# A planned transformer stack on one core: margins on landings, other luck numbers, waits for single pieces of preparation, later preparation of later layers

## The chip, the cores and the metric

The kernel runs on one core of one Trainium2 chip. The core has five engines with queues of their own: TensorE (PE, with its weight loads PEld), VectorE (DVE), ScalarE (ACT), GpSimd (POOL) and SyncE (SP), which here issues the DMAs. Each engine works off its queue in order; an instruction that waits for a semaphore holds up all that stand behind it. The metric is the time of one execution on the device in microseconds (us); the median of several runs is compared.

## The reference

The input x has 128 sequences of 64 tokens with 128 features; ctx has the same shape; cond is 128 by 128. Four layers of a conditioned transformer follow one another, all in fp32, with 16 heads of 8 features. In short:

```python
def adaln(x, scale, shift): return (1 + scale) * norm(x) + shift      # scale, shift from silu(cond) @ W + b

# layer 0: cross attention to ctx
x = x + attn(adaln(x), adaln(ctx)) @ Wp + bp
# layer 1: gated self attention, cross attention, gated GELU MLP
x = x + g1 * (self_attn(adaln(x)) @ W_proj + b)
x = x + cross_attn(norm(x), norm(ctx)) @ W_cproj + b
x = x + g2 * (gelu(adaln(x) @ W_mlp1 + b) @ W_mlp2 + b)
# layer 2: gated self attention, gated cross attention, gated SwiGLU MLP
x = x + g3 * (self_attn(adaln(x)) @ w_so + b)
s, i = top_k(scores(adaln(x), ctx), 16)            # 16 of 64 keys for each query and head
x = x + g4 * (softmax(s) @ v[i] @ w_co + b)
x = x + g5 * ((silu(a) * b) @ w_m2 + b_m2)         # a, b = adaln(x) @ w_m1 + b_m1
# layer 3: as layer 1
```

## The kernel before

The 128 sequences are cut into 16 chunks of 8 (512 tokens). Eight lanes each work on one chunk at a time, so the chunks go through in two waves. The function `chunk` writes down all steps of one chunk as operations: an engine, a cost in nanoseconds, the tiles that it writes and reads, a latency for a DMA, and a closure that issues the instructions.

One attention goes like this. A norm (statistics on DVE, L698; root on POOL, L711 and L712; normalisation on DVE, L719) is turned by PE (L686) and scaled on DVE (L728) and shifted on POOL (L729). PE makes keys (pk, L751), queries (pq, L757) and values (pv, L775), which ACT evicts. Four DMAs spread the queries (qbd, `spread`) so that PE can compute scores head by head (L809; for the top-k attention L839). ACT takes the exponential (L820), PE gathers the values (po, L939), ACT copies the result out (L949), and it takes a return trip through DRAM: store, load of the sums (`cs`), reciprocal on DVE (L974), store, broadcast load (`rb`), product on POOL (L984). Then PE makes the output product (py, L1049), which goes to the residual, with a gate that is fetched from DRAM by token (`by_token`). In the top-k attention DVE searches the 16 largest of 64 (L877, L879, L881), POOL masks (L907) and PE turns the result (ppt, L915). An MLP has products ph or pa and pg (L1071) and py (L1062).

The order of the instructions on every engine is made by the class `Plan` while the program is built. It keeps a clock for each engine, and at each turn gives out, of the operations within a window of each lane, the one that could start first; ties and near ties are moved by a jitter of 1% on each cost (`near`), drawn from the 21 numbers in `LUCK`, one for each 350 turns. An operation's start also takes in buffers (`start`; the pool `some` of 30 tiles, 3 query buffers, 4 value buffers, 8 probability buffers, PSUM banks), a table switch on ACT, a half-rate PE after idle stretches (`work`), the port that DVE and POOL share, DMAs that are still moving (`moves`, `moving`: each recent DMA adds its share to the landing of a new one) and the fetch of PE's code in blocks (`late`: before, the mean over eight phases of 256 instructions with a fetch of 3,400 ns, and for the small products of scores and gathers alone). `in_turn` then pins the order of each queue. Where the plan sees PE idle for over 1,000 ns ahead of a fresh PSUM tile, it issues filler matmuls over half of that time (`warm`, L1219 before), whose results are overwritten.

`prepare` is planned together with the lanes: it clears the query and value buffers on POOL, loads and turns the biases and the condition, makes the scales and shifts (pm, L532, L539), loads the weights (L557, L572; some are reordered on DVE, L391), the plain biases (pb, L508, L502, L579) and the gates (pg, L591; copies L598 to L601), which are stored in DRAM once (L609) and copied there in a 1 MB broadcast (L612). Each layer has a mark `ready[layer]`: a planned step without instructions that needs all parts of that layer, and `wop` lets each of the lane's steps that read weights wait for the mark. Preparation of layers 2 and 3 waits, in the plan, for the mark two layers earlier. Neither these marks nor the plan's times are instructions: on the chip a step waits for the tiles that it really reads.

At the end a count decides whether a second, slower network must run; it does not with these inputs.

Of the kernel before, what the change touches and what calls it, by code (L numbers as in the profile page):

```python
# [11 lines left out]
ALU = mybir.AluOpType  # L12
# [17 lines left out]
    14171, 51121, 34343, 55919, 69, 91271, 28258, 26931, 84363, 82916, 66128,  # L30
    83140, 28802, 5022, 44198, 77867, 32905, 75983, 99066, 65698, 73229,
# [68 lines left out]
PE, DVE, ACT, POOL, SP = "PE", "DVE", "ACT", "POOL", "SP"  # L100
# [30 lines left out]
class Plan:  # L131
# [15 lines left out]
    FETCH = 3400.0  # L147
    SHORT, LONG = 1500.0, 3500.0

    def __init__(self, tc, slots, warm, luck):  # L150
        self.tc, self.last, self.warm, self.luck = tc, {}, warm, luck
        self.count, self.chosen = 0, 0
        self.size = slots
        self.free = {kind: [(0.0, k) for k in range(n)] for kind, n in slots.items()}
        self.made, self.next_turn = {}, {}
        self.engine_free = dict.fromkeys((PE, DVE, ACT, POOL, SP), 0.0)
        self.port, self.active = {DVE: (0.0, 0.0), POOL: (0.0, 0.0)}, {}
        self.ops, self.holds, self.moving = None, None, []
        self.table = None
        self.small, self.blocks = 0, [(k, -self.FETCH) for k in range(0, self.BLOCK, 32)]  # L160
# [15 lines left out]
    def op(self, engine, cost, outs, ins, give, latency=0.0, bulk=False, table=None, small=0, within=False, port=False, moves=None, rate=1.0):  # L176
# [8 lines left out]
        o.moves, o.rate = moves, rate  # L185
# [12 lines left out]
    def start(self, o, first=True):  # L198
# [28 lines left out]
        if o.small:  # L227
            at += self.late(o, at)
# [17 lines left out]
    def late(self, o, at, keep=False):  # L246


        total = 0.0
        for k, (used, asked) in enumerate(self.blocks):  # L250
            waits, n = 0.0, o.small
            while used + n >= self.BLOCK:
                n -= self.BLOCK - used
                there = at + waits + o.cost * (1 - n / o.small)
                waits += max(0.0, asked + self.FETCH - there)
                used, asked = 0, max(there, asked + self.FETCH)
            total += waits
            if keep:
                self.blocks[k] = used + n, asked
        return total / len(self.blocks)  # L260
# [15 lines left out]
    def give_out(self, o, at):  # L276
# [19 lines left out]
        if fresh and idle > self.IDLE:  # L296
            self.work(at - idle, idle / 2)
        self.table = o.table or self.table
        if o.engine == PE:
            self.small = o.small  # L300
            if o.small:
                self.late(o, at, True)
# [7 lines left out]
        o.end = over + o.latency  # L310
        if o.moves:
            self.moving = [(t, n) for t, n in self.moving if over - t < self.LONG]
            o.end += sum(n[over - t >= self.SHORT] for t, n in self.moving)
# [32 lines left out]
    def run(self, lanes, count, ahead=()):  # L346
# [4 lines left out]
        while True:  # L351
# [9 lines left out]
            for n, ops in enumerate(todo):  # L361
                for i, (c, o) in enumerate(ops[: self.WINDOW]):
                    if o.missing or best and max(o.ready, self.engine_free[o.engine]) > best[0][0]:
                        continue
                    at = self.start(o, c == oldest or o.within)
# [13 lines left out]
def kernel(ctx: ExitStack, tc: tile.TileContext, ins: dict, out: bass.AP, nchunk: int = NCHUNK):  # L379
# [57 lines left out]
    def prepare(plan, ready, all_of_it, vblocks, queries, pool, spills):  # L437
# [7 lines left out]
        def clear(kind, cost, give):  # L445
            t = plan.tile(lambda: None, kind)
            op(POOL, cost, [t], [], lambda: give(t.slot))
            return t
# [6 lines left out]
        cleared = [clear("qbd", 1800, lambda k: nc.gpsimd.memset(queries[k], 0.0)) for _ in range(plan.size["qbd"])]  # L455
        cleared += [clear("values", 1500, clear_values) for _ in range(plan.size["values"])]
        if not all_of_it:
            op(SP, 1, ready, cleared, lambda: None)
# [26 lines left out]
        op(PE, 400, [ph], [bi, mb], turn_biases)  # L485
        op(DVE, 600, [biases], [ph], keep_biases)
        pc = mm("pc")
# [7 lines left out]
        op(PE, 220, [pc], [th], lambda: nc.tensor.transpose(pc()[:, :P], th(), ident))  # L495
# [15 lines left out]
        for layer in range(4):  # L511
            of, late = f"L{layer}", layer > 1
            dma, queue = (nc.sync, SP) if late else (nc.scalar, ACT)
            parts, weights, behind = cleared if layer == 0 else [], {}, [ready[layer - 2]] if late else []


            for key, wname, bname, kinds in CONDS:
# [3 lines left out]
                for i0 in range(0, len(kinds), 4):  # L521
# [5 lines left out]
                    ), 3500, bulk=late)  # L527
# [14 lines left out]
                    if those:  # L542
                        op(PE, 223 * len(those), [p], [cw, sc], products, bulk=late)
                        op(DVE, 350 * len(those), [done], [p, biases], keep, bulk=late)
                        parts.append(done)
                    weights[key, i0] = cw
# [3 lines left out]
            for name, k, n in WEIGHTS:  # L550
# [3 lines left out]
                ready_w[name] = whole = plan.kept(True)  # L554
                if m:
# [3 lines left out]
                    ), 3000, bulk=late)  # L559
# [7 lines left out]
                    parts.append(part)  # L567
                if m < n:
# [3 lines left out]
                    op(queue, 450, [whole], behind, lambda of_w=of_w, to=to: dma.dma_start(out=to, in_=of_w), 3000, bulk=late)  # L572
                    parts.append(whole)

            for name, w, b, bv in PLAIN:
                if name.startswith(of):
                    p, done = mm("pb"), plan.kept(True)
                    op(PE, 450, [p], [ready_w[w], bi, biases], lambda p=p, w=w, b=b, bv=bv: added(p()[:, :D], w, b, bv), bulk=late)
                    op(ACT, 300, [done], [p], lambda p=p, name=name: nc.scalar.copy(plain[name], p()[:, :D]), bulk=late)  # L579
                    parts.append(done)  # L580

            for n, (key, i, w, b, bv) in enumerate(GATES):
# [18 lines left out]
                op(PE, 900, [p], [cw, sc, bi, biases, *([ready_w[w]] if w else [])], products, bulk=late)  # L603
# [13 lines left out]
                ), 6000, bulk=late)  # L617
                parts.append(done)

            op(SP, 1, [ready[layer]], parts, lambda: None)  # L620
# [14 lines left out]
    def lane(n, plan, work, safe, acc, ready, vblocks, queries, pool, spills):  # L635
# [4 lines left out]
        op, layer = plan.op, [0]  # L640

        def wop(engine, cost, outs, takes, *rest, **how):

            op(engine, cost, outs, [*takes, ready[layer[0]]], *rest, **how)
# [35 lines left out]
        def flip(x, name):  # L680
# [7 lines left out]
            op(PE, 510, [p], [x], turn, rate=0.75)  # L688
# [38 lines left out]
        def modulate(h, pn, scale, shift, c):  # L727
            wop(DVE, 620, [h], [pn], lambda: nc.vector.tensor_tensor(b3(h()), b3(pn()), by_batch(scale, c), ALU.mult))  # L728
# [4 lines left out]
        def ln(x, eps, scale=None, shift=None, c=None):  # L733
# [5 lines left out]
            else:  # L739
                modulate(h, pn, scale, shift, c)  # L740
            return h, mv

        def attention(hq, hkv, wq, bq, wk, wv, topk=False):
# [7 lines left out]
            wop(PE, 890, [pk], [hkv], lambda: nc.tensor.matmul(pk(), lhsT=wk, rhs=hkv(), start=True, stop=True))  # L751
# [5 lines left out]
            wop(PE, 890, [pq, qbd, taken], [hq], lambda: nc.tensor.matmul(pq(), lhsT=wq, rhs=hq(), start=True, stop=True))  # L757

            qT = some([P, T])
            op(ACT, 670, [qT, qbd], [pq], lambda: nc.scalar.activation(qT(), pq(), AF.Identity, bias=bq))  # L760
# [16 lines left out]
            wop(PE, 930, [pv, vbuf], [hkv, taken], values)  # L777
# [48 lines left out]
            def weigh_rows(i, prs):  # L826
# [83 lines left out]
                for half, ex in enumerate(exs):  # L910
# [9 lines left out]
                    op(PE, 475, [ppt], [ex], turn, rate=0.75)  # L920
# [86 lines left out]
        def by_token(n, part, c, behind):  # L1007
# [9 lines left out]
            wop(SP, 590, [g], behind, fetch, 2690, moves=(395, 244))  # L1017
            return g

        def add(x, gate, c, parts):  # L1020

            if isinstance(gate, str):
                wop(POOL, 1265, [x], [x], lambda: nc.gpsimd.tensor_tensor(
# [18 lines left out]
        def project(oT, w, x, gate, c):  # L1042
# [3 lines left out]
            def product():  # L1046
                for t in range(NT):
                    cols = slice(t * P, (t + 1) * P)
                    nc.tensor.matmul(py()[:, cols], lhsT=oT()[:, cols], rhs=w, start=True, stop=True)  # L1049

            wop(PE, 960, [py], [oT], product)
            residual(py, x, gate, c, oT.behind)

        def mlp_out(gs, w2, x, gate, c):
# [3 lines left out]
            def sum_up():  # L1058
                for t in range(NT):
                    cols = slice(t * P, (t + 1) * P)  # L1060
                    for j in range(NJ):
                        nc.tensor.matmul(  # L1062
                            py()[:, cols], lhsT=gs[j // 2]()[:, j % 2, cols], rhs=w2[:, j, :], start=(j == 0), stop=(j == NJ - 1)
                        )

            wop(PE, 3610, [py], gs, sum_up)
            residual(py, x, gate, c, gs[1])

        def product(w, j, h, name, *takes):
            p = mm(name)  # L1070
            wop(PE, 890, [p, *takes], [h], lambda: nc.tensor.matmul(  # L1071
                p(), lhsT=w[:, j * P : (j + 1) * P], rhs=h(), start=True, stop=True
# [3 lines left out]
        def gelu_mlp(h, w1, b1, w2, x, gate, c):  # L1076
            gs = [shared([P, NJ // 2, T], "prob") for _ in range(2)]

            def part(j):
                ph = product(w1, j, h, "ph", *([] if j else gs))  # L1080
                op(ACT, 690, [gs[j // 2]], [ph], lambda: nc.scalar.activation(
# [7 lines left out]
        def swiglu_mlp(h, w1, b1, w2, x, gate, c):  # L1089
# [3 lines left out]
            def part(j):  # L1093
                pa = product(w1, j, h, "pa", *([] if j else gs))
                z, w = some([P, T]), some([P, T])
                op(ACT, 690, [z], [pa], lambda: nc.scalar.activation(z(), pa(), AF.Identity, bias=bvec(b1, j)))
                op(ACT, 580, [w], [pa], lambda: nc.scalar.activation(
# [14 lines left out]
        def chunk(c):  # L1112
            def qkv(w, b):
                w = W[w]
                return w[:, 0:D], bmix(b), w[:, D : 2 * D], w[:, 2 * D : 3 * D]

            def q_kv(wq, bq, wkv):
                w = W[wkv]
                return W[wq], bmix(bq), w[:, 0:D], w[:, D : 2 * D]
# [3 lines left out]
            def scaled(key, scale, shift):  # L1123
                return mods[key, scale], mods[key, shift], c
# [24 lines left out]
            layer[0] = 0  # L1149
# [5 lines left out]
            project(o, W["L0_xcond_Wp"], x, "L0", c)  # L1155

            layer[0] = 1
# [4 lines left out]
            project(o, W["L1_xcond_W_proj"], x, 0, c)  # L1162
# [4 lines left out]
            project(o, W["L1_xcond_W_cproj"], x, "L1c", c)  # L1167
            h, mv = ln(x, 1e-6, *scaled("L1", 4, 3))
            add(x, 1, c, mv)
            gelu_mlp(h, W["L1_xcond_W_mlp1"], "L1_xcond_b_mlp1", W["L1_xcond_W_mlp2"], x, 1, c)  # L1170

            layer[0] = 2
# [5 lines left out]
            project(o, W["L2_xcond_w_so"], x, 2, c)  # L1178
# [6 lines left out]
            project(o, W["L2_xcond_w_co"], x, 3, c)  # L1185
            h, mv = ln(x, 1e-6, *scaled("L2", 7, 6))
            add(x, 4, c, mv)
            swiglu_mlp(h, W["L2_xcond_w_m1"], "L2_xcond_b_m1", W["L2_xcond_w_m2"], x, 4, c)

            layer[0] = 3  # L1190
# [4 lines left out]
            project(o, W["L3_xcond_sa_proj_w"], x, 5, c)  # L1195
# [4 lines left out]
            project(o, W["L3_xcond_ca_proj_w"], x, "L3c", c)  # L1200
            h, mv = ln(x, 1e-6, *scaled("L3", 4, 3))
            add(x, 6, c, mv)
            gelu_mlp(h, W["L3_xcond_fc1_w"], "L3_xcond_fc1_b", W["L3_xcond_fc2_w"], x, 6, c)
# [7 lines left out]
    def network(lanes, safe, acc=None):  # L1211
# [13 lines left out]
        def planned(luck, tc=None, work=None, *tiles):  # L1225
            plan = Plan(tc, slots, warm, luck)
            tiles, ready = tiles or (None,) * 4, [plan.kept(True) for _ in range(4)]
# [74 lines left out]
```

## Time and profile before

| | |
|---|---|
| median of 3 runs | 1819.86 us (1807.23 to 1823.54) |
| the profiled execution | 1828.91 us |
| its span | 1827.1 us |
| its mean granted PE clock | 0.967 |
| DMA queue's bytes | 260.87 MB, 143 GB/s on average |

In the lines further down, a group's line has its line in the code, engine, operation, the tile written and the tiles read. A row of waits names the waiting engine, line and tile, then what ended the wait, with the total in us, the number of waits and the longest. The slices cut the span into 40 equal parts of 45.7 us with a busy share in tenths.

### The profile page before, as it was taken

The numbers are of one execution on the slowest core, as the hardware profiler recorded it, in microseconds if no ns is written. First come the engines' busy times: TensorE is split into PE (matmuls) and PEld (weight loads), VectorE is DVE, ScalarE is ACT, GpSimd is POOL, SyncE is SP. The second block draws the span as 40 slices with busy tenths as digits, with TensorE's granted clock in tenths as the row PEclk, the third lists the DMA queues.
The fourth block names the chain that finished last, engine by engine and source line by source line (L and its number), as shares of the span: only waits on it lengthen the run. The fifth ranks groups of instructions, "written<-read, shape, count | busy, mean of one in ns | idle before, by whom it ended". The sixth has DMA issues, their size and how long they took to land. (4 is left out here: it accounts for less than half of the span.)

```text
span 1827.1 us, 74911 instructions
## 1 busy us (share of the span) xinstructions
PE 1642.7 (90%) x30403; PEld 1149.1 (63%) x30403; DVE 1282.8 (70%) x6075; ACT 1248.3 (68%) x1824; POOL 1123.9 (62%) x1306
## 2 busy tenths in 40 slices
PE   6689999998887999998999999999999989889987
PEld 4456666666555666666666667676666666666665
DVE  5633344698999995966873596998684889996522
ACT  0477777587555777676777877787587768676562
POOL 6655465736655675755775666766666656576533
PEclk8899999999989999998999999999999999999999
DMA  8646655346422445446455545536354553345442
GB/s 248 190 143 183 174 161 158 104 131 184 115 68 84 119 125 157 146 142 180 132 157 156 152 128 174 166 117 176 102 162 141 149 149 112 114 123 144 118 142 85
DMA packets 296822, 260.87 MB, mean 143 GB/s; under 512 B 53196, under 2 KB 216212, under 8 KB 296468
## 3 DMA queue, kind: packets, MB, share of 16 engines
q1 hardware_dynamic: 296468, 255.99, 48.3%
q8 instruction: 242, 3.96, 1.0%
q14 instruction: 112, 0.92, 0.2%
HBM read 154.83 MB, written 79.04 MB: 128 GB/s over the span
## 5 line engine op out<-in xcount | busy, mean ns | idle before, releaser
L820 ACT ACTIVATE prob<-ps 128x1024 f32<-128x1024 f32 x384 | 375.4, 1024 | 86.2 <-PE ps L809 85.1
L939 PEld LDWEIGHTS po<-prob,vbuf 128*32 128x32 f32 x14336 | 221.3, 113 | 103.1 <-issue 56.1
L939 PE MATMUL po<-prob,vbuf 128*32 128x64 f32 x14336 | 262.3, 225 | 15.0 <-issue 10.7
L719 DVE TENSOR_SCALAR some<-x,parts,rstd 128x128 f32<-128x128 f32 x640 | 200.3, 376 | 66.0 <-POOL rstd L712 65.7
L907 POOL TENSOR_TENSOR some<-some,some 128x512 f32<-128x512 f32 x128 | 162.8, 1275 | 124.7 <-ACT some L899 80.7
L809 PE MATMUL ps<-qbd,some 32*64 32x256 f32 x6144 | 227.4, 393 | 11.0 <-DMA qbd<-some 5.7
L984 POOL TENSOR_TENSOR some<-some,some 128x512 f32<-128x512 f32 x112 | 143.2, 1279 | 125.8 <-DMA some<-spillrec 32.6
L712 POOL TENSOR_TENSOR rstd<-rstd,minus_half 128x4 f32<-128x4 f32 x192 | 201.6, 1050 | 16.0
L879 DVE MATCH_REPLACE8 some<-m,some 128x64 f32<-128x64 f32 x1024 | 206.5, 209 | 0.3 <-issue 0.3
L1037 POOL TENSOR_TENSOR x<-x,some 128x512 f32<-128x512 f32 x112 | 143.6, 1284 | 85.1 <-DVE some L1036 64.7
L782 ACT COPY vbuf<-pv 64x512 f32<-64x512 f32 x224 | 153.9, 687 | 44.8 <-PE pv L775 42.8
L877 DVE MAX8 m<-some 128x8 f32<-128x64 f32 x1024 | 172.0, 209 | 16.0 <-ACT some L857 15.8
L881 DVE MAX8 m<-some 128x8 f32<-128x64 f32 x1024 | 177.1, 215 | 0.0
L949 ACT COPY some<-po 128x512 f32<-128x512 f32 x224 | 132.0, 589 | 64.0 <-PE po L939 46.4
L1028 POOL TENSOR_TENSOR x<-x,some 128x512 f32<-128x512 f32 x112 | 142.0, 1273 | 52.1 <-DVE some L719 23.9
L809 PEld LDWEIGHTS ps<-qbd,some 32*64 32x64 f32 x6144 | 120.3, 133 | 64.4 <-issue 19.7
L1036 DVE TENSOR_TENSOR some<-py,some 128x512 f32<-128x512 f32 x112 | 76.4, 683 | 108.8 <-PE py L1049 56.5
L698 DVE BATCH_NORM_STATS2 parts<-x 128x6 f32<-128x256 f32 x320 | 120.8, 421 | 42.8 <-POOL x L1037 38.0
L729 POOL TENSOR_TENSOR some<-some,mod_L 128x512 f32<-128x512 f32 x112 | 117.3, 1050 | 36.5 <-DVE some L728 20.1
L686 PE MATMUL pn<-ident,some 128*128 128x128 f32 x768 | 127.4, 287 | 9.4 <-DVE some L719 2.8
L686 PEld LDWEIGHTS pn<-ident,some 128*128 128x128 f32 x768 | 92.5, 144 | 68.1 <-issue 20.5
L974 DVE RECIPROCAL rec<-sums 128x64 f32<-128x64 f32 x112 | 61.0, 545 | 97.1 <-DMA sums<-spill 96.8
(205 smaller groups left out, 3310.7 us busy)
## 6 DMA issues: line engine op xcount, KB each, us to landing
spill<-some SPq DMA_DIRECT2D x224, 256.0 KB
some<-gates SPq DMA_DIRECT2D x224, 256.0 KB
qbd<-some SPq DMA_DIRECT2D x448, 64.0 KB
some<-spill SPq DMA_DIRECT2D x112, 256.0 KB
some<-spillrec SPq DMA_DIRECT2D x112, 256.0 KB
some<-in_ctx_dram SPq DMA_DIRECT2D x48, 256.0 KB
gates<-once SPq DMA_DIRECT2D x7, 1024.0 KB
x<-in_x_dram SPq DMA_DIRECT2D x16, 256.0 KB
```

The costliest lines, as they stand in the source:

```text
L686: nc.tensor.transpose(p()[:, t * P : (t + 1) * P], x()[:, t, :], ident)
L712: nc.gpsimd.tensor_tensor(rstd(), rstd(), minus_half, ALU.pow)
L719: nc.vector.tensor_scalar(xn()[:, t, :], x()[:, t, :], mv()[:, t, 1:2], rstd()[:, t : t + 1], ALU.subtract, ALU.mult)
L782: nc.scalar.copy(v4(vbuf())[rows, :, :, 0 : 2 * HD].rearrange("p m h (d b) -> p m h d b", b=2)[:, :, :, :, b], pv()[rows].rearrange("p (m ...
L809: nc.tensor.matmul(pscs[g // 2]()[b * S : (b + 1) * S, g % 2, u].rearrange("p (h q) -> p h q", h=4), lhsT=kT()[rows, cols], rhs=qbd()[rows ...
L820: op(ACT, 975, [pr], [psc], lambda pr=pr, psc=psc: nc.scalar.activation(pr().rearrange("p g u h q -> p (g u h q)"), psc().rearrange("p g u ...
L877: nc.vector.max(m1()[:, j, :], ex()[:, j, :])
L879: nc.vector.match_replace(w()[:, j, :], m1()[:, j, :], ex()[:, j, :], GONE)
L881: nc.vector.max(m2()[:, j, :], w()[:, j, :])
L907: op(POOL, 1255, [ex], [ex, w], lambda ex=ex, w=w: nc.gpsimd.tensor_tensor(ex(), ex(), w(), ALU.mult), port=True)
L939: nc.tensor.matmul(po()[32 * j : 32 * j + 32, g, u], lhsT=vbuf()[:, at : at + 32], rhs=prs[gp]()[:, gi, u, j], start=True, stop=True,)
L1037: op(POOL, 1255, [x], [x, y], lambda: nc.gpsimd.tensor_tensor(x(), x(), y(), ALU.add), port=True)
```

## The change

The list of changes, in the order of the diff:

- `LUCK` has other numbers, so nearly every choice among near ties differs.
- `Plan` adds 200 ns (`MARGIN`) to the end of every operation that is not on PE, and three times (`WARY`) the share of moving DMAs to the end of a DMA.
- `late` follows one phase of PE's code blocks (starting at 63) for all PE operations, each with its count of instructions (`code`), with a fetch of 4,300 ns; fillers move the phase on.
- The steps of preparation may always take from the last four buffers of the pool `some`.
- The buffers that `prepare` clears are taken at once, in turns of a query and a value buffer, and no mark waits for all of them.
- The marks `ready` go. A dictionary `pieces` holds, for each weight, scale, gate, plain bias and for the biases, the planned pieces that make it, and each step of a lane waits in the plan for its own (`of`).
- The preparation of layers 1, 2 and 3 starts, in the plan, after a step on an engine `LATER` that has no instructions: 0, 8,000, 50,000 and 50,000 ns, added up layer by layer.
- The costs of the preparation's DMAs are 2,600 ns instead of 3,000 or 3,500, with shares of `moves`.

```diff
 LUCK = (
-    14171, 51121, 34343, 55919, 69, 91271, 28258, 26931, 84363, 82916, 66128,
-    83140, 28802, 5022, 44198, 77867, 32905, 75983, 99066, 65698, 73229,
+    1980, 16974, 8066, 5280, 77541, 15185, 58866, 59365, 80809, 90780, 79229,
+    45879, 3353, 2761, 99804, 35781, 81655, 65576, 25895, 83999, 21415,
 )
...
-PE, DVE, ACT, POOL, SP = "PE", "DVE", "ACT", "POOL", "SP"
+PE, DVE, ACT, POOL, SP, LATER = "PE", "DVE", "ACT", "POOL", "SP", "LATER"
+PREPARED = 0.0, 8000.0, 50000.0, 50000.0
...
-    FETCH = 3400.0
+    FETCH, AHEAD_OF_ALL = 4300.0, 63
     SHORT, LONG = 1500.0, 3500.0
+    WARY, MARGIN = 3.0, 200.0
...
-        self.small, self.blocks = 0, [(k, -self.FETCH) for k in range(0, self.BLOCK, 32)]
+        self.small, self.index, self.asked = 0, self.AHEAD_OF_ALL, -self.FETCH
...
-        if o.small:
+        if o.engine == PE:
             at += self.late(o, at)
...
-        total = 0.0
-        for k, (used, asked) in enumerate(self.blocks):
-            waits, n = 0.0, o.small
-            while used + n >= self.BLOCK:
...
-        return total / len(self.blocks)
+        total, left, asked = 0.0, o.code, self.asked
+        index = self.index
+        while index + left >= self.BLOCK:
+            left -= self.BLOCK - index
+            index = 0
+            there = at + total + o.cost * (1 - left / o.code)
+            total += max(0.0, asked + self.FETCH - there)
+            asked = max(there, asked + self.FETCH)
+        if keep:
+            self.index, self.asked = index + left, asked
+        return total
...
         if fresh and idle > self.IDLE:
             self.work(at - idle, idle / 2)
+            self.index += 4 * math.ceil(int(idle / 2 / 1.7) / 512)
...
-        o.end = over + o.latency
+        o.end = over + o.latency + (self.MARGIN if o.engine != PE else 0.0)
         if o.moves:
             self.moving = [(t, n) for t, n in self.moving if over - t < self.LONG]
-            o.end += sum(n[over - t >= self.SHORT] for t, n in self.moving)
+            o.end += self.WARY * sum(n[over - t >= self.SHORT] for t, n in self.moving)
...
-                    at = self.start(o, c == oldest or o.within)
+                    at = self.start(o, c in (oldest, -1) or o.within)
...
-        cleared = [clear("qbd", 1800, lambda k: nc.gpsimd.memset(queries[k], 0.0)) for _ in range(plan.size["qbd"])]
-        cleared += [clear("values", 1500, clear_values) for _ in range(plan.size["values"])]
+        for k in range(max(plan.size["qbd"], plan.size["values"])):
+            if k < plan.size["qbd"]:
+                clear("qbd", 1800, lambda k: nc.gpsimd.memset(queries[k], 0.0))
+            if k < plan.size["values"]:
+                clear("values", 1500, clear_values)
...
-            parts, weights, behind = cleared if layer == 0 else [], {}, [ready[layer - 2]] if late else []
+            parts, weights, behind = [], {}, []
+            if layer:
+                behind = [plan.kept(True)]
+                op(LATER, PREPARED[layer], behind, [], lambda: None)
...
-                    ), 3500, bulk=late)
+                    ), 2600, bulk=late, moves=(800, 450))
...
-                ), 6000, bulk=late)
+                ), 6000, bulk=late, moves=(3500, 3000))
                 parts.append(done)
-
-            op(SP, 1, [ready[layer]], parts, lambda: None)
+                pieces[n] = [done]
...
-        def wop(engine, cost, outs, takes, *rest, **how):
-
-            op(engine, cost, outs, [*takes, ready[layer[0]]], *rest, **how)
+        def of(*names):
+
+            return [t for name in names for t in pieces.get(name, ())]
...
-            wop(PE, 960, [py], [oT], product)
+            op(PE, 960, [py], [oT, *of(w)], product, code=4 * NT)
```

## The prediction

> **What bounds the kernel now.** I read the page first (totals, the span in slices), then the waits of PE, the stretches of time, the stretches of PE's filler matmuls alone, and PE's timeline at both ends.
>
> ```profile
> span 1827.1 us, 74911 instructions
> PE 1642.7 (90%) x30403; PEld 1149.1 (63%) x30403; DVE 1282.8 (70%) x6075; ACT 1248.3 (68%) x1824; POOL 1123.9 (62%) x1306
> ...
> PE   6689999998887999998999999999999989889987
> ...
> DVE  5633344698999995966873596998684889996522
> ```
>
> PE is busy 90% of the span and is the bound; its idle time lies at the front, at the end, and where DVE shows 9 (the top-k selection of the two waves of chunks).
>
> ```profile
> PE py L1049 <- POOL some L984: 26.4, 24, 2.7
> PE ps L839 <- issue: 17.5, 15, 2.1
> PE ppt L915 <- POOL some L907: 16.8, 19, 3.2
> PE po L939 <- issue: 10.7, 11, 2.5
> PE pb L508 <- DMA w_L_xcond_ca_proj_w<-n_L_xcond_ca_proj_w_dram: 9.5, 1, 9.5
> ```
>
> Columns: total us, times, longest. The largest wait is an output product that stands in PE's queue before its attention result is back from DRAM. "issue" is idle time without any awaited semaphore. The 9.5 us is preparation of layer 3 blocking PE.
>
> ```profile
> 0.00:140.00 140.00, 101.78 (x1627) 70.30 (x1635) 71.57 (x203) 59.84 (x84) 81.47 (x118) 0.90 0.65 195
> 300.00:700.00 400.00, 352.88 (x6325) 248.65 (x6324) 350.51 (x1954) 270.12 (x414) 246.59 (x272) 0.96 0.43 124
> 1700.00:1827.00 127.00, 108.84 (x1553) 73.48 (x1551) 39.91 (x92) 65.06 (x88) 54.76 (x65) 0.97 0.41 120
> ```
>
> Columns: the stretch, its length, busy PE, PEld, DVE, ACT, POOL, then granted clock. PE misses 38 us in the first 140, 47 in 300 to 700, 18 in the last 127. Fillers of L1219, which compute nothing, count as busy:
>
> ```profile
> 0.00:140.00 140.00, 7.50 (x10) 2.92 (x10) 0.90 0.65 195
> 300.00:700.00 400.00, 16.58 (x40) 7.64 (x40) 0.96 0.43 124
> sum 1827.00, PE 40.24 PEld 17.61; mean PE 6.71 PEld 2.93
> ```
>
> So 40 us more is filler. PE's timeline gives three places:
>
> ```profile
> 56.62 1.12 PE L809 MATMUL ps<-qbd,some 32*64 32x256 f32 x32
> 1764.01 1.16 PE L1049 MATMUL py<-w_L_xcond_sa_proj_w,some 128*128 128x128 f32 x8 [0.31 <-POOL some L984]
> 1786.56 0.65 PE L939 MATMUL po<-prob,vbuf 128*32 128x64 f32 x32 [0.22 <-ACT prob L820]
> 1802.68 1.05 PE L1049 MATMUL py<-w_L_xcond_ca_proj_w,some 128*128 128x128 f32 x8
> ```
>
> The first scores start only at 56.6 us; the last lane's self-attention product starts 63.1 us before the end; from the last gather's end (1787.2) to its product lie 15.5 us, the return trip through DRAM in a quiet stretch.
>
> **The change, part by part.** No waiting instruction is added: the "ready" marks and the LATER step emit nothing, the planner's margins are times inside it, and the chip waits for the tiles that a step really reads, as before. What changes is the order on each queue and the number of fillers. So I compare the orders of the two built programs. Work along an order is priced with the duration beside each step in the code; these add up to 1260.7 us for DVE against 1282.8 busy, so I use them for differences alone.
>
> *Front.* Before, PE has 24.0 us of work ahead of the first scores, so 32.6 of the 56.6 us are empty or filler. The timelines say why: on SP eight gate stores and the weight loads of layers 2 and 3 go ahead of the first query spread; on DVE the first context statistics stand behind layer 1's weight copies and start at 18.5; PE sits 5.3 us on layer 2's condition weights, then 3.6 on w_so. After, the loads of layers 2 and 3 stand behind the first lanes, the statistics come right behind layer 0's scales, and 9.0 us of PE work precede the first scores. Their time by rows: layer 0's scales end at 12.4; a copy and two statistics of 0.75 give 14.2; root on POOL 1.2; two normalisations of 1.1: 17.6; turn 0.6; scale 0.68 and shift 1.04: 20; query product 1.0, its eviction 0.7: 21.7; the spread's transfer (2.95 to 3.47 in the chain of waits) 25. The 3,432 filler columns ahead of the turn, at 2.36 ns each (40.24 us over 17,054 columns), cost 8.1 us and may push this to 28. At 27, 18.0 us are empty: 14.6 less. The 9.5 us on ca_proj goes too, but what is late next is DVE: in the first 50 us of PE work stand 52.7 us of DVE work (before 56.5). Of the 9.5 I take a third. Front: **-18** (-5 if DVE and POOL hold the lanes, -28 if all is gained). What moves later (15 us of preparation products, 20-odd loads, five 1 MB gate copies) costs PE the same time there; the loads lie under 150 GB/s stretches with DMA engines half idle.
>
> *Return trip.* In the order before, 21 of 112 output products stand under 16 us of PE work behind their last gather, which fits the 24 waits; after, 5 do, and the median distance goes from 18.4 to 24.8 us. Outside front and end those waits are 18.8 us in total; four fifths go: **-15** (0 if contention lengthens the trip as much, -19).
>
> *Top-k turns* (L915 behind POOL, 16.8 us): their distance at the 10th percentile goes from 12.9 to 17.0 us. But they stand where DVE binds, and PE then waits for something else: **-4** (0 to -12).
>
> *Code fetch.* The planner now follows one phase of 256-instruction blocks instead of a mean over eight. The 242 instruction packets of the queue table are 3.96 MB, 16 KB each. Blocks in which PE has under 3.7 us of work, the fastest fetches that the trace has bar a few (its 5th percentile of block intervals), fall short by 32.0 us in all before and 27.9 after, against 28.2 us of "issue" waits: **-4** (0 to -15). The Trainium skill, "Runtime: NRT & Kernel Launch", section Instruction fetch mechanics, speaks against this part: crossing a 16 KiB boundary is mostly hidden, since PE's buffer holds 2,048 instructions and issue is slower than refill. By it this term is 0 and the sum -17; the trace's 28.2 us of issue waits, lying 1 to 2 us behind the instruction packets' ends, disagree.
>
> *Top-k waves.* DVE is the bound there. The largest surplus of DVE over PE work along the order is 64.5 us in the first wave before (the trace: 47 idle and 16.6 filler in 300 to 700) and 74.5 after, since 28 of its 32 score steps stand closer together; second wave 32.6 before, about 27 after (two parts, 8 and 19). **+4** (-10 to +15).
>
> *Fillers.* 17,054 columns become 30,945: the padded landings let the planner see more idle time. Outside front and end it is 10,090 against 16,184, 14.4 us more; the nearest rows, the 16.6 us in the DVE-bound stretch, cost nothing as PE waited anyway, so half is on the path: **+7** (0 to +14).
>
> *ACT.* The order has six more table loads; at 1.28 us (the chain's row) 7.7 us on an engine that is 68% busy: 0 (up to 8 if each stood ahead of PE).
>
> *End.* Behind the last lane's self-attention product PE has 37.7 us of work before, 29.0 after. The lane's chain of 63.1 us does not shrink, so 8.7 us more of it is uncovered (its 10,206 filler columns, 24 us, fit into the 34 that are empty): **+9** (0 to +14).
>
> Sum: -18 -15 -4 -4 +4 +7 +9 = **-21 us**. The profiled execution took 1828.9 (span 1827.1), the median of three runs is 1819.9; a difference of orders applies to both, so 1819.9 - 21 = **1799**.
>
> **Rivals.** *Fillers on the path (slower).* The planner expects waits that do not come; its fillers stand ahead of ready work in an in-order queue. Place: the middle and the front's 3,432 columns. Price: all 13,891 added columns, 32.8 us in place of my 7, so 1825; it decides once less than about 11 us of them finds PE idle, and with front and return trip at half gain (+16) it reaches 1841. For: the middle's other distances hardly changed (products under 2 us behind what they need: 320 before, 299 after). Against: the fillers before stood where PE idled.
>
> *The gain is eaten where DVE binds.* Lanes that start 15 us sooner only reach the top-k wave sooner, and DVE's 74.5 us surplus takes the front's gain back: -21 + 18 = -3, so 1817. For: DVE 350 of 400 us busy. Against: PE is 93 to 95% busy in 700 to 1700, where time is PE's.
>
> *The clock.* The granted clock was 0.967, 60 us of full speed lost over the span, and 0.74 in 60 to 80 us, where PE was busy 9.8 of 20. Fewer gaps and 67 filler groups instead of 42 could win back a third to a half of it: 20 to 30 us on top, so about 1774. For: slow rows follow stalls. Against: slow stretches also stand where PE is busy (0.93 at 93% busy in 800 to 900). The Trainium skill, "TensorE: Matmul & The Clock Gate", Part 1, states that the clock is halved by default and released by about 3.4 us of activity; by that rule, the trace agrees, fillers pay.
>
> *The change does not do what it says:* excluded as a whole, since the orders differ on every queue.
>
> **How the numbers follow.** Changes under 1% (18 us) can't be told from none here: three runs spread over 16 us. Forecast 0.47, with its own range 1782 to 1812; the border is 1801.7, so 0.28 faster and 0.19 within. Clock 0.22, all faster. DVE eats it 0.10, within. Fillers 0.21: 0.17 slower than 1838, 0.04 within. Together faster 0.50, same 0.33, slower 0.17. The range takes the clock case's better half and the filler case up to its price: 1765 to 1842.
>
> **What would show it.** Right: first scores near 27 us, no wait over 3 us on preparation, output products' waits on POOL near 5 us in total, issue waits near 24, some 72 us of filler in all, the last self-attention product still some 63 us before the end. Wrong: idle in 300 to 700 well over 57 us; matmuls that follow a filler without any gap in 700 to 1700 (filler on the path); a front that still misses 38 us.

## The result and the profile after

The changed kernel took 1789.38 us (median of 4 runs, 1787.05 to 1796.32). The kernel before took 1821.7 beside it (4 runs, 1807.23 to 1825.91). The ratio, taken of the means, is 0.9843, with a 95% interval of 0.9803 to 0.9883. That is 29 us faster, and 32 by the medians, where 21 were forecast. The profiled execution of the changed kernel took 1796.32, its span is 1794.5, its granted clock 0.974.

The totals and the slices of the changed kernel's page:

```profile
span 1794.5 us, 75034 instructions
...
PE 1645.0 (92%) x30473; PEld 1146.3 (64%) x30473; DVE 1297.1 (72%) x6075; ACT 1257.5 (70%) x1830; POOL 1125.6 (63%) x1306
...
PE   7968999989988989999999999999999898899987
...
DVE  8524444589999999997445359899699987896412
```

DVE's first top-k wave is now an unbroken row of 9s, where before a 5 and two 6s broke it. PE is busy 2 us longer than before in a span that is 32.6 us shorter. The first two slices have risen from 6 and 6 to 7 and 9, but the third (90 to 135 us) shows a 6 where before stood an 8: something is given back there.

PE's waits in the changed kernel (total us, times, longest):

```profile
PE ps L823 <- DMA qbd<-some: 20.6, 9, 6.0
PE pk L765 <- POOL some L743: 14.2, 10, 7.9
PE ppt L929 <- POOL some L921: 13.6, 22, 1.9
PE py L1063 <- POOL some L998: 11.1, 12, 2.0
PE ps L853 <- issue: 6.6, 4, 2.3
PE po L953 <- ACT some L963: 6.5, 7, 3.0
PE po L953 <- issue: 5.8, 5, 2.7
```

The output products' wait on POOL (py) has fallen from 26.4 to 11.1 us, the two issue rows from 28.2 to 12.4. The block of 9.5 us on layer 3's weight is gone. Two of these rows have grown: the query spread (qbd) from 5.7 to 20.6 and the keys' input (pk) from 5.6 to 14.2.

The changed kernel by stretches (the stretch, its length, busy PE, PEld, DVE, ACT, POOL, granted clock, DMA share, GB/s):

```profile
0.00:140.00 140.00, 115.60 (x2043) 79.94 (x2043) 78.89 (x202) 74.60 (x102) 85.00 (x122) 0.93 0.68 197
...
300.00:700.00 400.00, 356.33 (x6331) 249.22 (x6324) 350.02 (x2023) 273.02 (x417) 244.38 (x264) 0.94 0.42 123
...
1667.00:1794.00 127.00, 108.88 (x1314) 75.07 (x1312) 33.32 (x75) 56.46 (x74) 46.37 (x54) 0.98 0.35 100
```

And its fillers of L1229 alone (the stretch, its length, PE, PEld, clock, DMA share, GB/s):

```profile
0.00:140.00 140.00, 12.27 (x26) 5.58 (x26) 0.93 0.68 197
...
300.00:700.00 400.00, 19.50 (x48) 8.94 (x48) 0.94 0.42 123
...
1667.00:1794.00 127.00, 19.83 (x54) 9.45 (x54) 0.98 0.35 100
sum 1794.00, PE 67.40 PEld 29.83; mean PE 11.23 PEld 4.97
```

The first 140 us miss 24 us instead of 38. In 300 to 700, idle and filler together are 43.7 + 19.5 = 63.2, as before (63.7): where DVE binds, nothing changed. In the last 127 us, PE without its fillers is busy 89.0, before 98.2.

**Where the 32 us came from.** A span is PE's idle time, its fillers and its own work. Before, 1827.1 = 184.4 + 40.2 + 1602.4; after, 1794.5 = 149.5 + 67.4 + 1577.6. Idle time fell by 34.9, but 27.2 of that was filled with matmuls that compute nothing. The other 24.8 us are the surprise: the same matmuls took less busy time. The granted clock says why. It was at half rate for 121.3 us of the span before and 93.7 after (the page's mean clock gives the same: twice the missing share of the span, 2 x 0.033 x 1827 = 121 and 2 x 0.026 x 1794 = 93). Of PE's busy time 103.4 and 72.9 us lay in it, 97.4 and 65.7 without the fillers. At half rate the same scores take about twice as long (2.01 us against 1.12 in the timeline below). So half of the last difference, 16 of the 24.8 us, is work that ran at full speed instead; the trace does not break down the other 9.

**When it came.** I add up PE's own work along each order, as the prediction did, and compare the times at which both kernels have done equally much of it. The changed kernel leads by 29.8 us after 60 us of work, by 14.0 after 80 (126 us in its own time), by about 12 after 200 and by 11.7 after 600, by 25.5 after 700, by 39.2 after 1400 and by 32.3 at the end. So the front gained 30 and lost half of it at once. Twelve came between 650 and 700 of work, where before had a stretch of 10 us at a clock of 0.50 (856 to 866 us); most of the rest came by 1400.

PE's timeline of the changed kernel at the first scores, at the two long waits and at the last self-attention product (start, length, line, tiles; in brackets the idle time ahead and what ended it):

```profile
27.95 1.12 PE L823 MATMUL ps<-qbd,some 32*64 32x256 f32 x32 [0.88 <-DMA qbd<-some]
...
95.87 2.01 PE L823 MATMUL ps<-qbd,some 32*64 32x256 f32 x32 [5.46 <-DMA qbd<-some]
...
114.51 2.07 PE L765 MATMUL pk<-some,w_L_xcond_W_qkv 128*128 128x512 f32 x2 [7.92 <-POOL some L743]
...
1729.12 1.06 PE L1063 MATMUL py<-w_L_xcond_sa_proj_w,some 128*128 128x128 f32 x8
```

The first scores start at 27.95 us instead of 56.6. The last self-attention product starts 65.4 us before the end, before 63.1. Between them stand two new waits of 5.5 and 7.9 us, and the same place by stretches of 10 us:

```profile
80.00:90.00 10.00, 9.75 (x263) 6.63 (x265) 1.15 (x2) 9.03 (x13) 2.93 (x5) 1.00 0.50 108
90.00:100.00 10.00, 4.54 (x75) 3.18 (x65) 0.08 (x1) 2.52 (x3) 1.26 (x1) 0.66 0.77 254
100.00:110.00 10.00, 6.59 (x206) 4.84 (x204) 2.49 (x7) 6.82 (x9) 2.42 (x4) 1.00 0.78 245
110.00:120.00 10.00, 5.49 (x16) 3.19 (x20) 1.55 (x3) 1.27 (x2) 4.58 (x7) 0.51 0.60 179
```

In 90 to 100 no engine is busy even half the time but the DMA engines, which move 254 GB/s; PE waits for a query spread, and that the other engines wait for transfers too is read from this and not from each wait. The clock follows with 0.66 and 0.51. SP's timeline names the newcomers, the 1 MB gate copies of layer 2:

```profile
85.21 0.58 SPq L624 DMA_DIRECT2D gates<-once  x1
...
94.85 0.60 SPq L624 DMA_DIRECT2D gates<-once  x1
...
101.67 0.59 SPq L624 DMA_DIRECT2D gates<-once  x1
```

Before, these three were issued at 50 and 63 us, where PE had less to lose (9.8 of 20 us busy in 60 to 80).

### The profile page after: what moved, and what is told of

Its sections match the earlier page's. It is cut to its first block, busy times and chain, and to the rows that moved or that the text cites. A ratio compares the mean times of both kernels' runs of the same rounds, so it can differ in the third digit from the quotient of the medians.

```text
span 1794.5 us, 75034 instructions
## 1 busy us (share of the span) xinstructions
PE 1645.0 (92%) x30473; PEld 1146.3 (64%) x30473; DVE 1297.1 (72%) x6075; ACT 1257.5 (70%) x1830; POOL 1125.6 (63%) x1306
## 5 line engine op out<-in xcount | busy, mean ns | idle before, releaser
L953 PEld LDWEIGHTS po<-prob,vbuf 128*32 128x32 f32 x14336 | 216.1, 111 | 106.5 <-issue 54.1
L953 PE MATMUL po<-prob,vbuf 128*32 128x64 f32 x14336 | 256.1, 223 | 15.9 <-ACT some L963 6.5
L731 DVE TENSOR_SCALAR some<-x,parts,rstd 128x128 f32<-128x128 f32 x640 | 207.9, 387 | 55.8 <-POOL rstd L724 55.2
L823 PE MATMUL ps<-qbd,some 32*64 32x256 f32 x6144 | 227.6, 393 | 22.2 <-DMA qbd<-some 20.6
L1042 POOL TENSOR_TENSOR x<-x,some 128x512 f32<-128x512 f32 x112 | 143.1, 1281 | 55.1 <-DVE some L731 28.1
L796 ACT COPY vbuf<-pv 64x512 f32<-64x512 f32 x224 | 153.9, 687 | 29.2 <-PE pv L789 27.2
L698 PE MATMUL pn<-ident,some 128*128 128x128 f32 x768 | 122.8, 282 | 9.2 <-DVE some L731 2.9
L698 PEld LDWEIGHTS pn<-ident,some 128*128 128x128 f32 x768 | 89.5, 142 | 62.5 <-issue 18.8
L742 DVE TENSOR_TENSOR some<-pn,mod_L 128x512 f32<-128x512 f32 x112 | 75.7, 682 | 61.9 <-PE pn L698 46.5
```

The lines of the kernel that those rows point to most:

```text
L698: nc.tensor.transpose(p()[:, t * P : (t + 1) * P], x()[:, t, :], ident)
L731: nc.vector.tensor_scalar(xn()[:, t, :], x()[:, t, :], mv()[:, t, 1:2], rstd()[:, t : t + 1], ALU.subtract, ALU.mult)
L796: nc.scalar.copy(v4(vbuf())[rows, :, :, 0 : 2 * HD].rearrange("p m h (d b) -> p m h d b", b=2)[:, :, :, :, b], pv()[rows].rearrange("p (m ...
L823: nc.tensor.matmul(pscs[g // 2]()[b * S : (b + 1) * S, g % 2, u].rearrange("p (h q) -> p h q", h=4), lhsT=kT()[rows, cols], rhs=qbd()[rows ...
L953: nc.tensor.matmul(po()[32 * j : 32 * j + 32, g, u], lhsT=vbuf()[:, at : at + 32], rhs=prs[gp]()[:, gi, u, j], start=True, stop=True,)
```

## The experiments

My theory after the result: the new order shortens the waits that the prediction named, and the fillers win more by the clock than they cost. The rivals: the fillers cost time and the order is worth more than 32 us; the gate copies take back the front's gain; the draw of `LUCK` alone makes the difference.

### Fillers: none, in both kernels, and more of them

The order of all else stays; the filler matmuls are left out, in the changed kernel and in the one before.

```diff
-            if fresh and idle > self.IDLE:
-                self.in_turn(lambda: self.warm(fresh(), idle / 2))
```

> The changed kernel with every step in the same order on each queue, but without its filler matmuls (30,945 columns, 67.4 us of PE busy time). Theory 'fillers lie on the path' (the prediction's term of +7 us, its slower rival 24 to 33 us): the time falls by 5 to 30 us against the changed kernel, to 1760 to 1785. Theory 'fillers hold the clock' (PE busy at half rate fell from 103 to 73 us although idle time only fell by 35): half-rate time rises by 30 us or more and the time rises by 10 us or more. If they only fill time in which PE waits anyway: within 5 us of 1789, half-rate time up a little.

> The kernel before, in its own order, without its filler matmuls (17,054 columns, 40.2 us busy). 'On the path': 3 to 16 us faster than before. 'Fillers hold the clock': slower than before by 5 us or more, half-rate time over 123 us. Hidden: within 5 us.

Measured: the changed kernel without fillers took 1802.78 us (10 runs), 0.9954 of before (0.9934 to 0.9973); before without fillers 1815.67 (10 runs), 1.0020 (1.0000 to 1.0041). With fillers the changed kernel is at 0.9843 and, run again, 0.9819. So its fillers save 1.1 to 1.35% of 1811 us, 20 to 24 us. Those two ratios come from other groups of runs, where the kernel before took about 10 us longer, and the plain medians differ by only 13 to 16 us. The one changed kernel with fillers on the same chip is that with the gate copies held back, in the next part: 23 us faster, of which some 4 are the copies', so 19. The fillers of before save about 4 us there, with an interval that begins at 0: by the time that is 'hidden', though half-rate time rises without them as 'hold the clock' has it. The span and the mean clock of the changed kernel without fillers, then its stretch of the first wave:

```profile
core 0: 1799.8 us, clock 0.962
```

```profile
300.00:700.00 400.00, 342.41 (x6371) 241.94 (x6370) 344.35 (x1992) 272.38 (x415) 239.18 (x259) 0.92 0.42 122
```

Half-rate time rises to 136.1 us, and PE's own work takes 1610.0 us instead of 1577.6. Without fillers the two kernels agree in this (136.7 and 1611.3 before). So the 24.8 us by which the same matmuls became cheaper belong to the fillers, not to the order. What the order alone is worth is the ratio of the two kernels without fillers: 1802.78 against 1815.67, 13 us.

Then the other way, in the same order again, with three quarters of the foreseen idle time filled instead of half:

```diff
-                self.in_turn(lambda: self.warm(fresh(), idle / 2))
+                self.in_turn(lambda: self.warm(fresh(), idle * 0.75))
```

> The changed kernel with fillers over three quarters of each foreseen idle stretch instead of half, all else in the same order. 'Fillers hold the clock, and more is better': half-rate time falls under 90 us and the time by 3 to 10 us. 'Half is about as much as there is room for': the added 34 us of filler stand partly ahead of ready work, and the time rises by 3 to 15 us although half-rate time falls.

Measured: 1782.28 us (5 runs), 0.9789 (0.9757 to 0.9821). Beside it on the same chip the changed kernel itself was run again:

> The changed kernel once more, beside the next three on the same chip: 0.980 to 0.988 of before.

Measured: it took 1787.25 (6 runs), 0.9819 (0.9785 to 0.9853), at a clock of 0.980 and with 70.3 us at half rate, so the first profile, the slowest of its four runs, had an unlucky clock. More filler is some 5 us faster; the intervals overlap, but half-rate time and PE's own work agree. The same two views for three quarters:

```profile
core 0: 1779.9 us, clock 0.983
```

```profile
300.00:700.00 400.00, 361.28 (x6514) 252.23 (x6507) 356.37 (x2052) 275.60 (x422) 248.88 (x270) 0.97 0.43 124
```

In this stretch the clock is 0.92 without filling, 0.94 and 0.97 in the two profiles with half, and 0.97 with three quarters; the second step is not clear of the difference between two profiles of one program. DVE gets more of its work done in the same 400 us (344.35; 350.02 and 352.38; 356.37), though no DVE instruction was touched. In all, filler of 0, 67 to 69 and 91.6 us goes with half-rate time of 136, 70 to 94 and 61 us, and with 1610, 1570 to 1578 and 1562 us for the same own work.

One sign by which the prediction wanted to know fillers on the path is there all the same: all 14 groups of fillers between 700 and 1700 us are followed by a matmul without any gap (4 of 5 before). So some of them do hold up ready work; the kernels without fillers show that the clock pays back more than that.

### The gate copies held back

The order of all else stays, and the 1 MB copies of layers 2 and 3 go to SP only after so many further DMA steps:

```diff
+HOLD = {2: 20, 3: 45, 4: 150, 5: 40}
...
+            if o.hold:
+                self.held.append((self.issued + o.hold, o.give))
...
+            self.issued += o.engine == SP
+            for h in [h for h in self.held if h[0] <= self.issued]:
+                self.held.remove(h)
+                self.in_turn(h[1])
...
-                ), 6000, bulk=late, moves=(3500, 3000))
+                ), 6000, bulk=late, moves=(3500, 3000), hold=HOLD.get(n, 0))
```

> The changed kernel with the same order of everything, except that the 1 MB gate copies of layers 2 and 3, of which three stand within 17 us at 85 to 102 us, are issued further apart (20, 45 and 150 DMA steps later, one of layer 3 40 later). Theory 'the copies collide with the lanes' round trips' (the lead over the kernel before falls from 30 to 14 us between 85 and 126 us): the waits of 5.5 and 7.9 us there go, the lead stays over 22 us at 150 us of PE work, and the time falls by 5 to 14 us, to 1775 to 1784. Theory 'the first lanes run into a dry stretch whatever the copies do' (all lanes have finished layer 0 at once): the waits stay or move, and the time is within 4 us of 1789.

> The changed kernel with the gate copies further apart, beside the changed kernel itself. The waits of 5.5 and 7.9 us at 90 to 115 us were gone in its first profile. If the copies' collision is the cause and is worth what was expected, it is 5 to 14 us faster than the changed kernel in this comparison; within 4 us, and the collision costs nothing that lasts.

Measured: 1780.01 us (4 runs), 0.9817 (0.9787 to 0.9847); again, beside the changed kernel on one chip, 1783.29 (6 runs), 0.9789 (0.9757 to 0.9822) against its 0.9819. The first lies in the range of 1775 to 1784, but on a chip where the kernel before is some 10 us faster too. Side by side it is 4 us, or 0.3%, with intervals that overlap, and less than the 5 to 14 expected. In the first profile the layer-2 copies are issued at 99.51, 132.04 and 258.76 us, so one of them still falls into the crowded place:

```profile
99.51 0.54 SPq L633 DMA_DIRECT2D gates<-once  x1
```

So the run spreads the copies out, and does not take them away. PE's waits between 60 and 140 us, first held back, then held back again:

```profile
PE py L1072 <- POOL some L1007: 4.4, 2, 2.4
PE pk L774 <- POOL some L752: 3.9, 1, 3.9
```

```profile
PE py L1072 <- POOL some L1007: 6.9, 2, 4.7
PE ps L832 <- DMA qbd<-some: 4.1, 3, 1.9
```

The two long waits of 5.5 and 7.9 (13.4 us) shrink to 4.1 in all in the first profile and 4.4 in the second (rows of 0.2 and 0.3 are not shown), but output products wait in their place. The stretches of the first profile show it:

```profile
90.00:100.00 10.00, 7.93 (x158) 5.44 (x143) 2.57 (x7) 5.55 (x8) 3.68 (x5) 0.83 0.71 200
100.00:110.00 10.00, 6.14 (x112) 4.06 (x111) 1.56 (x3) 4.72 (x7) 4.59 (x7) 0.86 0.84 253
110.00:120.00 10.00, 9.62 (x286) 7.20 (x289) 4.40 (x12) 6.83 (x9) 4.58 (x6) 0.97 0.68 197
```

Between 60 and 140, PE is busy 69.8 and 67.6 us instead of 65.5 and 66.9. The lead over the kernel before is 23 to 24 us after 80 us of work, instead of 14 to 17; after 150 it is 11 instead of 5 to 7, where over 22 was expected. So most of the lead goes even with the copies spread, as the theory of a dry stretch has it. Crowding the copies costs some 4 us that last, which is not clear of noise in the time. Whether the rest is lost to the lanes' own transfers stays open, since one copy still moves in 100 to 110, where the DMA engines carry 253 GB/s.

### The draw of luck, and the margins

Four kernels cross the planners with other numbers: the changed planner with the old 21 numbers, the old one with the new 21, and each with `LUCK = (0,)`. A fifth keeps the change and its numbers but takes the margins out:

```diff
-    WARY, MARGIN = 3.0, 200.0
+    WARY, MARGIN = 1.0, 0.0
```

> The changed kernel with the luck numbers of before. Theory 'the model of the plan makes the gain' (margins, code phase, preparation): 1780 to 1800, as the changed kernel. Theory 'the drawn numbers make it': 1810 to 1840, as before or worse. In between: both have a share.

> The kernel before with the luck numbers of the changed kernel; its filler columns come to 46,514 where its own numbers give 17,054, so its plan foresees far more idle time. If a plan with numbers that were not chosen for it is simply a bad draw, 1860 to 1920, as the changed plan with the old numbers (1914 us, 62,177 columns). If the new numbers were good in themselves: 1790 to 1830.

> The changed kernel with MARGIN 0 and WARY 1, the new luck numbers kept; 35,385 filler columns where the changed plan has 30,945. Theory 'margins make the order robust': output products' waits on POOL go from 11 back to 20 us or more. Theory 'the draw decides': the plan is another draw, 1840 to 1930, whatever its waits are, with the time lying in a drawn order that leaves PE dry.

> The changed kernel with the single luck number 0, an order that nobody chose; 47,856 filler columns. As the other draws that were not chosen: 1860 to 1930. If the changed planner is better in itself, it lies under the planner of before with the same number by 20 us or more.

> The kernel before with the single luck number 0; 37,878 filler columns. 1850 to 1950. Together with the two crossed runs (1914 for the changed planner, 1950 for the old one) it says whether the changed planner is better on orders that were not chosen.

Measured, with PE's waits for output products on POOL and all its waits for issue:

| planner, numbers | us (runs) | ratio, 95% | py on POOL, us / times | issue, us |
|---|---|---|---|---|
| before, its own | 1819.86 (3) | 1 | 26.4 / 24 | 29.9 |
| before, new | 1950.15 (4) | 1.0700 (1.0658 to 1.0742) | 31.2 / 23 | 23.0 |
| before, 0 | 1908.55 (2) | 1.0487 (1.0423 to 1.0550) | 35.1 / 26 | 14.7 |
| changed, its own | 1789.38 (4) | 0.9843 (0.9803 to 0.9883) | 11.1 / 12 | 13.9 |
| changed, old | 1913.64 (4) | 1.0560 (1.0516 to 1.0604) | 15.0 / 12 | 13.3 |
| changed, 0 | 1842.53 (2) | 1.0124 (1.0065 to 1.0183) | 21.4 / 16 | 10.7 |
| changed without margins, new | 1919.51 (4) | 1.0547 (1.0497 to 1.0598) | 34.3 / 24 | 10.0 |

The changed planner with the old numbers was expected at 1780 to 1840, the one before with the new ones at 1790 to 1830 or 1860 to 1920; both came out worse. The changed planner with 0 came out better than its 1860 to 1930. Each planner does 53 to 130 us worse with other numbers than its own. That its own were picked by trying many is a guess from this; no run shows how they were found. The numbers are not good or bad in themselves: those that give 1789 with the changed planner give 1950 with the old one. So the time of a single draw says little about a planner, and the fifth kernel's 1919.51 is no price of the margins. With the number 0 for both, the changed planner is 66 us faster, and with numbers not its own its two draws (1843, 1914) are ahead of the old one's (1909, 1950) on average; two draws each don't settle it.

The waits are steadier than the times. The row of output products, of the old planner with the new numbers, of the changed one with the old, and of the changed one without margins:

```profile
PE py L1049 <- POOL some L984: 31.2, 23, 5.8
```

```profile
PE py L1063 <- POOL some L998: 15.0, 12, 3.7
```

```profile
PE py L1063 <- POOL some L998: 34.3, 24, 6.5
```

With margins this wait is 11 to 21 us in three draws, without them 26 to 35 in four, the changed planner without margins among them: the margins do this, in every draw tried. Taking the fillers out leaves it so, with 14.1 us in the changed order and 24.2 in that of before. The 9.5 us block on layer 3's weight is in all three orders of the old planner (9.5, 9.7, 9.6) and in none of the changed one. What the bad draw of the old planner loses, it loses late. The time that passes beyond PE's own work, as added up along each order, is, after 700 us of work, 199 before, 173 after and 184 for the old planner with the new numbers; at the end it is 323, 290 and 447.

### Both at once

Copies held back and three quarters filled:

> The changed kernel with the gate copies further apart and fillers over three quarters of each foreseen idle stretch. Each alone gave 0.9789 of before, against 0.9819 for the changed kernel. If the two are independent: about 0.976, 1774 to 1781; if both fill the same empty time: 0.978 to 0.980.

Measured: 1778.77 us (4 runs, 1775.37 to 1789.98), 0.9790 (0.9732 to 0.9847), at a clock of 0.985 with 55.1 us at half rate. It has the lowest median of all and beats before by 2.1%; but each edit alone reached 0.9789, so that the two add up is not shown.

## Why the prediction was right, and where it was not

The time lay inside the range and inside the forecast's own range, and the change is faster by more than 1%. Part of that is luck: the sum came near because two errors of opposite sign nearly cancelled. The terms other than the fillers added up to -28; without fillers in either kernel the order is worth -13. The fillers were put at +7; they gained 19 to 24 us against some 4 before, so the term is about -15 to -20.

- **Front, -18.** The mechanism held: first scores at 27.95 where 27 was worked out, the block on ca_proj gone, 30 us of lead. The step that failed is that what moves later "costs PE the same time there; the loads lie under 150 GB/s stretches with DMA engines half idle". The mean of a stretch was the wrong number: where the copies landed, 245 to 254 GB/s moved, and 16 us of the lead were gone at 126 us. What stayed is 14 there and about 12 after 200 us of work, of a range of 5 to 28. One reading of the front was short: by SP's timeline 14 gate stores, not eight, go ahead of the first query spread before (8 at 21.85 us, 6 at 42.51); the sum does not use the count.
- **Return trip, -15.** Right in kind: the wait fell by 15.3 us in all, and with the margins it is shorter in every draw tried. Outside front and end it fell from 18.8 to 9.2, so by 10, as 12 products still wait (11.1 us) where 5 us were forecast.
- **Top-k turns, -4.** From 16.8 to 13.6: -3.2.
- **Code fetch, -4.** Mis-sized: issue waits of 24 us were forecast, 13.9 are left of 29.9, a fall of 16, just beyond the end of the range at -15. The three draws of the changed planner have 11 to 14 us and that without margins 10, those of the old one 15 to 30. But without fillers the same two orders have 19.6 us after and 16.6 before. So the order alone does not shorten these waits; they change with the fillers in it, and how is not shown. Block distances in the order foresaw 32.0 and 27.9 and so missed most of the fall. As to the rule that was weighed (the Trainium skill, "Runtime: NRT & Kernel Launch", section Instruction fetch mechanics: crossing a boundary is mostly hidden), the trace went on disagreeing: waits of 10 to 30 us exist in every draw. How much of their fall reached the end was not tried by itself.
- **Top-k waves, +4.** Idle and filler in 300 to 700 stayed at 63 us: 0.
- **Fillers, +7.** Wrong in sign. The count was right (72 us forecast, 67.4 found). The step that failed is "half is on the path", which priced them by the time they occupy and left out the clock, though the clock rival stood further below. That rival named the mechanism and gave 20 to 30 us; the runs show it, at 19 to 24 for all fillers. It erred in adding them to a whole gain of 21 and came out at 1774. The rule named with it (the Trainium skill, "TensorE: Matmul & The Clock Gate", Part 1: halved by default, released by activity) is borne out here: half-rate time falls from 136 to 61 us as filler rises from 0 to 91.6.
- **ACT, 0.** ACT's busy time rose by 9.2 us, about the 7.7 counted; whether any of it reached the path was not tried.
- **End, +9.** Right: in the last 127 us PE does 9.2 us less of its own work (98.2 to 89.0) under a lane's chain of 65.4 us.
- **The other rivals.** Fillers on the path: fallen as a price, as taking them out makes the kernel slower, though its sign, no gap behind a filler, is there. The gain eaten where DVE binds: fallen, as the lead is about 12 us after 200 us of work and again after 600; in between it swings from 1 to 31.
- **What was not weighed.** An order drawn with other numbers differs by 53 to 130 us from the one that came with its planner. No term or rival had this; the comparison of the two orders, step by step, took its place and was right in most steps.

## What to carry to other kernels

On an engine whose clock follows its activity, price a filler by what it does to the clock of the work behind it, not by the time it takes; a build without it, in both kernels, separates that from the order. Before counting a moved transfer as free, look at the 10 us around its new place, not at the mean of the stretch. And when a planner and its random choices change together, compare waits across several draws: they show what the planner does, while the time of one draw mostly shows the draw.

## What the runs showed of the hardware

- Matmuls that compute nothing pay for themselves: from half (the second profile) to three-quarter filling, 23 us more of filler (68.8 to 91.6) went with a span that is 5 us shorter, 20 us less idle time and 8 us less for the same own work.
- The clock moves from run to run by itself: the same program had 93.7 and 70.3 us at half rate in two profiles, with spans of 1794.5 and 1784.6.
- With 1 MB copies issued at 85.21 and 94.85 us among the lanes' transfers, every computing engine was busy less than half of the 10 us from 90 to 100 (PE 4.54, DVE 0.08, ACT 2.52, POOL 1.26) while 254 GB/s moved.
